# A two-layer Mamba, attention and expert network: instructions ordered by a planner inside the kernel, pairs of scan states added on GpSimd, expert weights in shared buffers

## The chip, the cores and the metric

The kernel runs on one core of one Trainium2 chip. The core has five engines that run side by side, each with an instruction queue that is worked off in order: TensorE (PE, the matrix unit), VectorE (DVE), ScalarE (ACT), GpSimd (POOL) and SyncE (SP), which here only issues DMA transfers. The time is the device time of one execution in microseconds. Three runs of the kernel before gave 986.20, 989.38 and 991.23 us; their median, 989.38 us, is the time to beat.

## What is computed

The input `x` is (4, 512, 128): four batches of 512 tokens with 128 features. Every part is added to its own input:

```python
x = x + L0_attn(layernorm(x), ...)   # selective scan, then attention and a gated FFN
x = x + L0_ffn(layernorm(x), ...)    # 128 -> 512 -> 128, ternary weights, exact gelu, layernorm
x = x + L1_attn(layernorm(x), ...)   # a second selective scan
x = x + L1_ffn(layernorm(x), ...)    # router with top 1 of 8 experts, 128 -> 2 x 512 -> 128
```

The selective scan appears twice per batch, once in each layer. It projects x to 256 inner channels and a gate of the same width, convolves four steps in time, and then runs a recurrence for 256 channels times 16 states:

```python
h = exp(delta_t * A) * h + delta_t * B_t * x_t      # h: 256 channels x 16 states
y_t = sum over the 16 states of h * C_t
```

`y` gets a skip term, is multiplied by `silu(gate)` and projected back to 128 features. In the expert layer every token goes through the one expert with the highest router probability, and the result is multiplied by that probability.

## The kernel before

**Layout.** A batch lies as four tiles of 128 tokens, or transposed as 128 features by 512 tokens. The 256 inner channels are two chunks of 128 partitions. Both layers' scans go through `scan_states` (L455), four batches times two layers: eight scans.

**One scan** is 16 jobs, a job being one chunk and two states (`NG = 2`). A job is fed by `feed` (L463): TensorE spreads the row B of each state over 128 partitions into a PSUM tile `b_n` (L469; the weight is one column of `sel`, broadcast), ScalarE makes `decay = exp(delta * A)` (L473), and SP loads the two rows of C, spread over 128 partitions, into `rep` (L478; 512 KB each). Then VectorE multiplies `b_n` by `du` (L509) and runs the recurrence as one scan instruction per state into `hs` (L510). GpSimd multiplies the pair by C in one instruction of 128x1024 (L511). At last `drain` (L485) sums over the states: TensorE multiplies each of the two halves of `hs` by the identity matrix and accumulates in the PSUM tile `y` (L494), one float32 matmul of 512 columns per state. Such a matmul is two passes in the trace, so 256 of them show as 512 records. `drain` of job k-1 stands behind the recurrence of job k, and it is held behind the last `spread` matmul by `issue_after`. The buffers are 3 for `b_n`, 3 for `decay`, 3 for `rep`, 3 for `hs` and 1 for `y`.

**The other stages** of a batch are generators: `front0` and `front1` (norm, transposition, convolution, gate, delta), `first` (the end of scan 0, then attention over four heads with 12 groups of query tiles), `dense` (gated FFN, then the ternary FFN), `second` (the end of scan 1, router). Batches 0 and 1, and 2 and 3, form two groups. For a group, `sort` gives every token a row in a DRAM table so that each expert's tokens fill whole tiles of 128, and writes the tokens there by eight indirect DMAs from the GpSimd queue (L783). `experts` then goes through 15 tiles: load a tile `xg` (L801), read the number of its expert into an SP register (L804), load its weights as `w_up`, 512 KB with two buffers, and `w_dn`, 256 KB with three (L809), normalise, transpose, multiply, and write the rows back with one indirect DMA (L832). The weight loads are held behind the last load of `rep`.

**The order of the work.** `run` gives each generator a due time and a length in units of one scan (scan 0 of batch b is due at b, scan 1 at 4+b, attention of b at b+1, and so on), and `issue` (L909) always advances the generator that is due first. This writes the program in one order; the framework's scheduler, with its own durations, then moves instructions within each engine's queue. Some of its freedom is taken away by hand: `behind` (issue after another instruction), `when` (wait for another instruction), and a hand-placed load of the exponential table on ScalarE at the end of each convolution (L408). ScalarE holds the tables for one set of functions at a time. Exp and Ln share a set here; Silu and Gelu each need another.

Of the kernel before, what the change touches and what calls it, by code (L numbers as in the profile page):

```python
# [8 lines left out]
F32 = mybir.dt.float32  # L9
# [9 lines left out]
P = 128  # L19
# [34 lines left out]

class Net:


    def __init__(self, ctx, tc, a, out):
        self.tc, self.nc, self.a, self.out = tc, tc.nc, a, out
        pool = lambda name, bufs, **k: ctx.enter_context(tc.tile_pool(name=name, bufs=bufs, **k))  # L60
# [13 lines left out]
    def c(self, name, shape, dtype=F32):  # L74
        return self.const.tile(shape, dtype, tag=name, name=name)

    def t4(self, name, bufs=None):
        return self.tok.tile([P, NT, D], F32, tag=name, name=name, bufs=bufs)

    def ft(self, name, shape, bufs=None, tag=None):  # L80
        return self.feat.tile(shape, F32, tag=tag or name, name=name, bufs=bufs)
# [4 lines left out]
    def behind(self, ins):  # L86
        return nullcontext() if ins is None else self.tc.issue_after(ins.ins)

    def when(self, done, ins):

        self.tc.add_manual_dep(
            ins.ins, done.ins.name,
            mybir.DependencyInfo(mybir.DependencyClass.Sync, mybir.DependencyReason.DATA),
        )

    def mm(self, name):
        return self.p_mm.tile([P, T], F32, tag="mm", name=name)

    def mm4(self, name):
        return self.p_mm.tile([P, NT, D], F32, tag="mm", name=name)  # L100

    def sm(self, name, shape, bufs=None):
        return self.small.tile(shape, F32, tag=name, name=name, bufs=bufs)
# [15 lines left out]
    def setup(self):  # L119
# [6 lines left out]
        make_identity(nc, self.ident)  # L126
# [32 lines left out]
    def setup_rest(self):  # L159
# [3 lines left out]
        make_causal_mask(nc, self.causal, mask_val=NEG)  # L163
# [69 lines left out]
        self.sorted = []  # L233
        for k, rows in enumerate(GROUPS):
            n = len(rows) * NT + E - 1
            d = self.dram.tile([n * P, XW], F32, tag=f"sorted{k}", name=f"sorted{k}", bufs=1)
            for j in range(0, n, NX):
                m = min(NX, n - j)
                nc.sync.dma_start(
                    out=d[j * P:(j + m) * P, :].rearrange("(j p) d -> p j d", p=P), in_=zero[:, :m, :]  # L240
                )
            self.sorted.append(d)
# [57 lines left out]
    def load_x(self, b):  # L300
        self.rows_x[b] = self.tok.tile([P, NT, XW], F32, tag="x", name=f"x_{b}", bufs=B)
# [50 lines left out]
    def rmsnorm(self, name, x, behind=None):  # L352
# [6 lines left out]
        with self.behind(behind):  # L359
            for t in range(NT):  # L360
                nc.scalar.activation(y[:, t, :], x[:, t, :], AF.Identity, scale=r[:, t:t + 1])
# [16 lines left out]
    def front(self, b, layer, x, scale=None):  # L378
# [10 lines left out]
        conv, gate = [], []  # L389
        for c in range(NB):  # L390
            ps = self.mm("conv_ps")
            for k in range(KC):
                last = nc.tensor.matmul(  # L393
                    ps, lhsT=taps[:, k, c * P:(c + 1) * P], rhs=xpad[:, k:k + T],
                    start=(k == 0), stop=(k == KC - 1),
# [4 lines left out]
        for c, ps in enumerate(conv):  # L400
            self.when(last, nc.scalar.activation(xs[:, c, :], ps, AF.Silu, bias=cb[:, c:c + 1]))
        for c in range(NB):
            ps = self.mm("z_ps")
            last = nc.tensor.matmul(ps, lhsT=wz[:, c * P:(c + 1) * P], rhs=xT, start=True, stop=True)
            gate.append(ps)
        for c, ps in enumerate(gate):
            self.when(last, nc.scalar.activation(sz[:, c, :], ps, AF.Silu))
        self.tc.keep_in_program_order(nc.scalar.preload_act_table_set("natural_log_exp_and_others"))  # L408
# [10 lines left out]
        cd = self.dram.tile([NS, T], F32, tag="cd", name="cd")  # L419
        nc.sync.dma_start(out=cd, in_=crow[32:32 + NS, :])  # L420

        parts = self.feat.tile([P, T], BF16, tag="parts", name="parts")
# [32 lines left out]
    def scan_states(self, b, layer):  # L455
# [7 lines left out]
        def feed(k):  # L463
# [3 lines left out]
            for i in range(NG):  # L467
                t = self.p_b.tile([P, T], F32, tag="b_n", name="b_n")
                spread = nc.tensor.matmul(t, lhsT=self.sel[:, n + i:n + i + 1].to_broadcast([P, P]), rhs=parts, start=True, stop=True)  # L469
# [7 lines left out]
            rep = self.scan.tile([P, NG, T], F32, tag="rep", name="rep", bufs=3)  # L477
            self.rep = nc.sync.dma_start(  # L478
# [4 lines left out]
            self.spread = spread  # L483

        def drain(k):  # L485

            c, n = jobs[k]
            if n == 0:
                y[c] = self.p_y.tile([P, T], F32, tag="y", name="y")
                nc.tensor.matmul(y[c], lhsT=skip[:, c, :], rhs=xs[:, c, :], start=True, stop=False)  # L490
            hs = done[k]
            with self.behind(self.spread):
                for i in range(NG):
                    nc.tensor.matmul(  # L494
                        y[c], lhsT=self.ident, rhs=hs[:, i, :],
                        start=False, stop=(n + i == NS - 1),
                    )
# [5 lines left out]
        for k, (c, n) in enumerate(jobs):  # L503
# [3 lines left out]
            hs = self.scan.tile([P, NG, T], F32, tag="hs", name="hs", bufs=3)  # L507
# [3 lines left out]
            nc.gpsimd.tensor_tensor(hs, hs, rep, ALU.mult)  # L511
            done[k] = hs
            if k >= 1:
                drain(k - 1)
            yield
        drain(len(jobs) - 1)
# [16 lines left out]
    def front0(self, b):  # L533
        with self.behind(self.backs.get(self.fronts - 2)):
            self.h[b], x = self.two_norms(self.x[b])
# [6 lines left out]
    def back0(self, b):  # L542
        h = self.h[b]
        self.backs[len(self.backs)] = self.nc.vector.tensor_tensor(h, h, self.back(b, 0), ALU.add)

    def attention(self, b):
        nc = self.nc
        h = self.h[b]
        x = self.rmsnorm("a", h, self.last_head)
# [20 lines left out]
        for tiles in ((0, 1), (2,), (3,)):  # L570
            for hd in range(HEADS):
# [6 lines left out]
                last = turned[-4] if len(turned) >= 4 else None  # L578
                for n, i in enumerate(tiles):
                    nk, k0 = (i + 1) * P, at[n] * P  # L580
                    with self.behind(last):
                        nc.tensor.matmul(  # L582
# [394 lines left out]
```

## Time and profile before

The profiled execution took 989.92 us, of which the span from its first to its last instruction is 988.1 us.

| engine | busy us | share of span | what it mostly does |
|---|---|---|---|
| PE | 807.4 | 82% | 281.1 us of it are the matmuls of `hs` by the identity (L494) |
| DVE | 660.1 | 67% | recurrence 302.4 us (L510), product by `du` 168.1 us (L509) |
| ACT | 572.1 | 58% | decay 177.6 us (L473), 100 table loads of 1283 ns |
| POOL | 460.1 | 47% | `hs` by C 305.7 us (L511) |
| DMA | | 30.3% of 16 engines | 102.24 MB, 103 GB/s in the mean |

A busy share says how long an engine had an instruction in work, not that it set the pace. Matmuls overlap each other and their weight loads (PEld), and the mean duration of one is longer than the distance between two starts. The granted TensorE clock was 0.911 of full speed in the mean.

The trace splits into six stretches, which are used below: 0 to 50 us (loads and the first front part, before the first recurrence at 50.5 us), 50 to 150 us (scans and front parts only), 150 to 640 us (attention and dense parts beside the scans), 640 to 750 us (the last front parts and the sorting of the first group), 750 to 890 us (the last scans beside the experts of the first group), and from 890 us on (router and experts of the second group, alone).

### The profile page before, as it was taken

How to read it: one execution, taken by the hardware profiler on the slowest of the kernel's cores; microseconds unless marked ns; L12 is line 12 of the kernel's file. 1: busy time of each engine (PE TensorE's matmuls, PEld its weight loads, DVE VectorE, ACT ScalarE, POOL GpSimd, SP SyncE). 2: the span in 40 equal slices, each digit the busy share in tenths (PEclk: the TensorE clock that was granted, in tenths of full speed). 3: DMA queues.
4: the chain of work that ended last, by engine and by line, in shares of the span. 5: the costliest groups of instructions: out<-in, count | busy, mean ns of one | idle time of the engine just before them, and what ended most of it. 6: DMA issues, size and time to landing. Idle time of an engine off the chain costs nothing. (4 is left out here: it accounts for less than half of the span.)

```text
span 988.1 us, 10337 instructions
## 1 busy us (share of the span) xinstructions
PE 807.4 (82%) x3242; PEld 450.1 (46%) x3242; DVE 660.1 (67%) x1111; ACT 572.1 (58%) x938; POOL 460.1 (47%) x305
## 2 busy tenths in 40 slices
PE   3876779997899988999989989789585987982685
PEld 1322244443444554544644446344332555641675
DVE  2399876876668586678774768757666878872122
ACT  4474356745669566686674864568445666841332
POOL 4256752553534454336442444444455845663122
PEclk9978989998899799998998979899797998995799
DMA  5236421222212121121320212121025574732463
GB/s 147 76 109 171 144 87 66 85 107 85 86 49 99 46 86 64 65 87 64 107 75 33 79 50 98 73 86 66 30 97 175 176 233 145 230 99 75 160 217 113
DMA packets 44084, 102.24 MB, mean 103 GB/s; under 512 B 6660, under 2 KB 18912, under 8 KB 44030
## 3 DMA queue, kind: packets, MB, share of 16 engines
q1 hardware_dynamic: 42558, 99.45, 30.3%
q0 software_dynamic: 1472, 2.14, 0.6%
q8 instruction: 25, 0.41, 0.2%
q14 instruction: 29, 0.24, 0.1%
HBM read 97.14 MB, written 5.34 MB: 104 GB/s over the span
## 5 line engine op out<-in xcount | busy, mean ns | idle before, releaser
L511 POOL TENSOR_TENSOR hs<-hs,rep 128x1024 f32<-128x1024 f32 x128 | 305.7, 2389 | 313.8 <-DVE hs L510 156.4
L510 DVE TENSOR_TENSOR_SCAN hs<-decay,b_n 128x512 f32<-128x512 f32 x256 | 302.4, 1207 | 3.6 <-ACT decay L473 1.8
L494 PE MATMUL y<-hs,ident 128*128 128x512 f32 x512 | 281.1, 662 | 13.1 <-POOL hs L511 13.1
L473 ACT ACTIVATE decay<-delta,nega 128x511 f32<-128x511 f32 x256 | 177.6, 717 | 111.1 <-DVE hs L510 89.2
L509 DVE TENSOR_TENSOR b_n<-b_n,du 128x512 f32<-128x512 f32 x256 | 168.1, 687 | 44.8 <-PE b_n L469 35.5
L494 PEld LDWEIGHTS y<-hs,ident 128*128 128x128 f32 x512 | 100.9, 210 | 129.1 <-issue 82.0
L469 PE MATMUL b_n<-parts,sel 128*128 128x512 bf16 x256 | 92.1, 408 | 61.2 <-DVE hs L510 56.8
L393 PE MATMUL conv_ps<-xpad,taps 128*128 128x512 f32 x128 | 62.7, 619 | 3.1 <-ACT xpad L374 2.6
L855 DVE TENSOR_TENSOR sa<-sa,g_ps 128x512 f32<-128x512 f32 x30 | 20.5, 684 | 66.3 <-PE g_ps L852 59.2
L591 ACT ACTIVATE pr<-s_ps,nm 128x128 f32<-128x128 f32 (+2 forms) x64 | 33.5, 524 | 53.8 <-DVE nm L590 52.5
L832 POOL DMA_INDIRECT out<-yj,xg x30 | 29.9, 996 | 63.0 <-DVE yj L829 60.3
L602 PEld LDWEIGHTS tp<-v,pT 128*128 128x128 f32 x320 | 43.6, 203 | 32.8 <-ACT pT L598 19.4
L369 PE MATMUL tp<-ident,ln 128*128 128x128 f32 x96 | 25.0, 335 | 37.5 <-ACT ln L330 20.8
L582 PE MATMUL s_ps<-kT,qT 32*128 32x128 f32 (+3 forms) x128 | 55.1, 511 | 0.0
L469 PEld LDWEIGHTS <-sel 128*128 128x128 bf16 x256 | 26.5, 107 | 58.1 <-issue 56.4
L602 PE MATMUL tp<-v,pT 128*128 128x33 f32 x320 | 45.6, 285 | 2.1 <-ACT pT L598 2.1
L369 PEld LDWEIGHTS tp<-ident,ln 128*128 128x128 f32 x96 | 14.3, 160 | 66.1 <-ACT ln L330 22.3
L595 PEld LDWEIGHTS tp<-ident,pr 128*128 128x128 f32 x160 | 21.0, 152 | 50.1 <-ACT pr L591 39.0
L845 PE MATMUL a_ps<-xj,w_up 128*128 128x128 f32 x240 | 36.4, 297 | 8.9 <-ACT xj L817 8.7
L811 ACT ACTIVATE xn<-xg 128x128 f32<-128x128 f32 x30 | 14.8, 494 | 48.8 <-DMA xg<-sorted 48.6
L595 PE MATMUL tp<-ident,pr 128*128 128x128 f32 x160 | 32.0, 303 | 13.0 <-ACT pr L591 12.5
L590 DVE TENSOR_REDUCE nm<-s_ps 128x1 f32<-128x128 f32 (+2 forms) x64 | 30.7, 479 | 17.3 <-PE s_ps L585 15.5
(201 smaller groups left out, 1254.1 us busy)
## 6 DMA issues: line engine op xcount, KB each, us to landing
rep<-cd SPq DMA_DIRECT2D x128, 512.0 KB, 3.6
w_up<-in_w_rows SPq DMA_DIRECT2D x30, 512.0 KB, 4.5
w_dn<-in_w_rows SPq DMA_DIRECT2D x30, 256.0 KB, 4.5
xg<-sorted SPq DMA_DIRECT2D x30, 66.0 KB, 2.3
sorted<-zero SPq DMA_DIRECT2D x2, 726.0 KB, 8.6
x<-in_x SPq DMA_DIRECT2D x4, 256.0 KB, 4.4
raw_cw<-in_cw_rows SPq DMA_DIRECT2D x2, 512.0 KB, 4.6
sorted<-zero SPq DMA_DIRECT2D x2, 264.0 KB, 10.1
```

The lines of the kernel that those rows point to most:

```text
L369: nc.tensor.transpose(ps[:, t * P:(t + 1) * P], x[:, t, :], self.ident)
L393: last = nc.tensor.matmul(ps, lhsT=taps[:, k, c * P:(c + 1) * P], rhs=xpad[:, k:k + T], start=(k == 0), stop=(k == KC - 1),)
L469: spread = nc.tensor.matmul(t, lhsT=self.sel[:, n + i:n + i + 1].to_broadcast([P, P]), rhs=parts, start=True, stop=True)
L473: nc.scalar.activation(da[:, i, 1:], delta[:, c, 1:], AF.Exp, scale=neg_a[:, c * NS + n + i:c * NS + n + i + 1],)
L494: nc.tensor.matmul(y[c], lhsT=self.ident, rhs=hs[:, i, :], start=False, stop=(n + i == NS - 1),)
L509: nc.vector.tensor_tensor(b, b, du[:, c, :], ALU.mult)
L510: nc.vector.tensor_tensor_scan(hs[:, i, :], da[:, i, :], b, 0.0, ALU.mult, ALU.add)
L511: nc.gpsimd.tensor_tensor(hs, hs, rep, ALU.mult)
L582: nc.tensor.matmul(ps[:, k0:k0 + nk], lhsT=qT[hp, i * P:nk], rhs=kT[hp, :nk], start=True, stop=False)
L595: last = nc.tensor.transpose(tp[:, j * P:(j + 1) * P], pr[:, j * P:(j + 1) * P], self.ident)
L602: nc.tensor.matmul(tp[:, n * w:(n + 1) * w], lhsT=pT[:, (at[n] + j) * P:(at[n] + j + 1) * P], rhs=v[:, j, g, :], start=(j == 0), stop=(j = ...
L845: nc.tensor.matmul(pa[:, f, :], lhsT=w[0][:, f * P:(f + 1) * P], rhs=xj, start=True, stop=True)
```

## The change

Three things are edited; the arithmetic is otherwise the same.

1. **The planner.** `self.nc` is now a recorder. Every call is kept as an `Op` with its engine, the boxes of the tiles it reads and writes, and a duration by a formula in `Plan.cost`. A tile is a `Slot` in a ring of buffers that is only made when its first instruction is emitted. When everything is collected, `Plan.order` plays all five queues forward: of the first 60 ready instructions of each engine it takes the one that can start first (within 0.1 us, the one with the earlier due time), allowing for free buffers, for 1.35 us at a change of function table, and for DMA at 200 GB/s. `Plan.issue` emits in that order; the framework's scheduler is switched off for all engines but GpSimd, whose instructions are chained one behind the other, except for a group of indirect DMAs of one kind. The hand-made `behind`, `when` and the hand-placed table load go; a table load is emitted where the planned order changes the set. Where the recorder counts instructions, ScalarE has 57 table loads instead of 100, all other counts of the old instructions on TensorE, VectorE and ScalarE are as before save for those of point 2, and SP has 90 weight loads instead of 60.
2. **Pairs of states.** After the multiplication by C, GpSimd adds the second half of `hs` to the first (128 new instructions of 128x512), and TensorE accumulates one matmul per job instead of two. `hs` has 4 buffers instead of 3, and job k is drained in its own step.
3. **Expert weights.** `w_up` and `w_dn` lose buffers of their own. The two halves of the first weight (256 KB each, two loads instead of one) use the buffers of attention's `pT`, now 4 instead of 3, and the second weight those of `pr` (4).

In addition the convolution waits for the end of the scan two front parts earlier (`after=back`), where before the norm ahead of it stood behind that instruction, and the counting matmuls of `sort` wait for the router's last choice.

```diff
+    def cost(self, engine, what, out, ins, args, k):
+        n = width(out)
+        m = max([n] + [width(v) for v in ins])
+        if engine == "tensor":
+            if what == "transpose":
+                return 0.112
+            half = k["rhs"].slot.dtype == BF16 if isinstance(k["rhs"], View) else False
+            return max(0.11, n * 0.00042) if half else 2 * max(0.112, n * 0.000836)
+        if engine == "scalar":
+            scalars = sum(isinstance(k.get(x), View) for x in ("bias", "scale", "accum_out"))
+            return 0.21 + n * 0.00083 + 0.1 * scalars
+        if engine == "vector":
+            if what == "tensor_tensor_scan":
+                return 0.2 + n * 0.002
...
+            return 0.19 + m * 0.001
+        if engine == "gpsimd":
+            if ALU.pow in args:
+                return 1.15
+            return 0.3 + n * (0.00215 if what == "tensor_tensor" else 0.001)
+        return 0.45
...
+            best = None
+            for e, ops in ready.items():
+                found = []
+                for op in ops[:60]:
+                    at = room(op)
+                    if at is None:
+                        continue
+                    at = max(at, op.at, free[e])
+                    if op.table and op.table != table:
+                        at += self.SWITCH
+                    found.append((at, op))
+                if found:
+                    first = min(f[0] for f in found)
+                    at, op = next(f for f in found if f[0] <= first + 0.1)
+                    if best is None or at < best[0]:
+                        best = at, op
...
             hs = done[k]
-            with self.behind(self.spread):
-                for i in range(NG):
-                    nc.tensor.matmul(
-                        y[c], lhsT=self.ident, rhs=hs[:, i, :],
-                        start=False, stop=(n + i == NS - 1),
-                    )
+            nc.tensor.matmul(y[c], lhsT=self.ident, rhs=hs[:, 0, :], start=False, stop=(n + NG == NS))
...
-            hs = self.scan.tile([P, NG, T], F32, tag="hs", name="hs", bufs=3)
+            hs = self.scan([P, NG, T], F32, tag="hs", name="hs", bufs=4)
...
             nc.gpsimd.tensor_tensor(hs, hs, rep, ALU.mult)
+            nc.gpsimd.tensor_tensor(hs[:, 0, :], hs[:, 0, :], hs[:, 1, :], ALU.add)
             done[k] = hs
-            if k >= 1:
-                drain(k - 1)
+            drain(k)
...
-            w = self.ft("w_up", [P, 2 * EF], bufs=2), self.ft("w_dn", [P, EF], bufs=3)
-
-            with self.behind(self.rep):
-                for part, name in zip(w, ("w1_rows", "w2_rows")):
-                    nc.sync.dma_start(out=part, in_=self.a[name][bass.ds(e, 1)].rearrange("o p n -> (o p) n"))
+            w = []
+            for name, at, tag in (("w1_rows", 0, "pT"), ("w1_rows", EF, "pT"), ("w2_rows", 0, "pr")):
+                part = self.ft("w_" + name, [P, EF], bufs=4, tag=tag)
+                get = nc.add(
+                    "sync", lambda p=part, n=name, at=at: weights(p, n, at, e), [part], [], 0.45, after=[e]
+                )
+                get.bytes = 4 * P * EF
+                w.append(part)
```

## The prediction

> **What bounds the kernel now.** No engine is full over the whole span (PE 82%, DVE 67%), so the first view is the busy time of each engine by stretch. Columns: length, then busy us (instructions) of PE, PEld, DVE, ACT and POOL, then clock, DMA share and GB/s.
>
> ```profile
> 0.00:50.00 50.00, 30.41 (x71) 13.76 (x72) 17.02 (x50) 23.35 (x42) 18.00 (x48) 1.00 0.37 110
> 50.00:150.00 100.00, 73.15 (x184) 31.37 (x184) 88.22 (x113) 51.05 (x87) 60.94 (x31) 0.86 0.41 130
> 150.00:640.00 490.00, 445.04 (x1716) 237.13 (x1715) 349.06 (x604) 318.28 (x540) 219.86 (x122) 0.92 0.21 75
> 640.00:750.00 110.00, 85.86 (x293) 42.09 (x292) 71.48 (x128) 65.44 (x95) 51.87 (x33) 0.91 0.22 76
> 750.00:890.00 140.00, 115.35 (x568) 74.53 (x566) 112.63 (x159) 89.02 (x126) 85.62 (x46) 0.94 0.54 177
> 890.00:988.10 98.10, 57.57 (x417) 51.27 (x417) 21.69 (x63) 25.01 (x53) 23.81 (x25) 0.82 0.45 142
> ```
>
> TensorE sets the pace for half of the kernel: from 150 to 640 us it is busy 445.0 of 490 us, 91%, while DVE has 71% and POOL 45%. From 50 to 150 us it is DVE (88%). From 750 to 890 us PE and DVE share it (82% and 80%). From 640 to 750 us nothing is above 78%: the work waits for chains. After 890 us there is one chain only.
>
> The groups by cost say what this work is (after the bar: busy us and mean ns of one; then the idle time of the engine before it).
>
> ```profile
> L511 POOL TENSOR_TENSOR hs<-hs,rep 128x1024 f32<-128x1024 f32 x128 | 305.7, 2389 | 313.8 <-DVE hs L510 156.4
> L510 DVE TENSOR_TENSOR_SCAN hs<-decay,b_n 128x512 f32<-128x512 f32 x256 | 302.4, 1207 | 3.6 <-ACT decay L473 1.8
> L494 PE MATMUL y<-hs,ident 128*128 128x512 f32 x512 | 281.1, 662 | 13.1 <-POOL hs L511 13.1
> L509 DVE TENSOR_TENSOR b_n<-b_n,du 128x512 f32<-128x512 f32 x256 | 168.1, 687 | 44.8 <-PE b_n L469 35.5
> ```
>
> A third of PE's time is L494, which only sums. POOL waits 313.8 us before L511: it has room. DVE waits only 44.8 us before L509.
>
> **The change, part by part.**
>
> *Half of L494 goes.* 256 of its 512 records, at 281.1/512 = 0.549 us of busy time each, are 140.5 us: 20.1 in 50–150, 77.8 in 150–640 (half of 155.6 us in that stretch), 14.7 in 640–750, 27.9 in 750–890. Where PE sets the pace, the next bound is what is late next.
>
> *128 adds on POOL.* L645 is the same operation and shape:
>
> ```profile
> L645 POOL TENSOR_TENSOR x<-x,h x4: 1262/1263/1267, 275.4 to 658.7; 128x512 f32<-128x512 f32 x4
> L510 DVE TENSOR_TENSOR_SCAN hs<-decay,b_n x256: 1184/1209/1222, 50.5 to 883.4; 128x512 f32<-128x512 f32 x128
> L509 DVE TENSOR_TENSOR b_n<-b_n,du x256: 668/689/700, 49.3 to 881.6; 128x512 f32<-128x512 f32 x128
> L297 DVE SCALAR_TENSOR_TENSOR tern_fc<-raw_fc,thr_fc,low_fc x1: 2812/2812/2812, 39.2 to 39.2; 128x512 f32<-128x512 f32 x1
> ```
>
> 128 x 1.263 = 161.7 us. By jobs in each stretch (20, 69, 13, 26) POOL becomes 86, 307, 68 and 118 us. A job then costs POOL 2.39 + 1.26 = 3.65 us and DVE 2 x (0.687 + 1.207) = 3.79 us: nearly equal. The add also lies between recurrence and `y`; with four `hs` buffers it delays `y`, not the next job, as long as POOL's queue keeps up.
>
> *A rule against this.* The Trainium skill (Perfetto Trace Analysis, Optimizing Scalar/DVE Operations) warns that GpSimd and DVE share an SBUF read port, so moving work between them may not help. If each add held off DVE for its length, DVE would rise by 161.7 us to 822 us, and the gain would be gone. The four rows above decide: recurrence and product hardly vary (1184 to 1222 ns, 668 to 700 ns) although POOL is busy half of the time; both read one operand from PSUM. L297, two operands from SBUF, took 2.81 us where its twin for the other weight took 0.72. It started 0.1 us after a 2.35 us POOL instruction. So only the few DVE instructions with two SBUF operands pay: over L256, L297, L348, L446 and L449 the excess over their shortest is some 11 us. With POOL busy about 70% instead of half in the middle I add 5 us (0 to 15), and not 161.7.
>
> *Table loads.* ACT has 43 fewer, at 1.283 us: 55 us less of 572. ACT is no bound (65% from 150 to 640), so I count nothing by itself; the attention chain gets shorter, which helps to reach the next bound. Worth 0 to 15 us.
>
> *The planner.* Its durations stand close to the rows: recurrence 1.22 us (trace 1.207), product 0.70 (0.687), `hs` by C 2.50 (2.389), add 1.40 (1.263), table 1.35 (1.283). One is short: a float32 matmul of 512 columns is 0.856 us, while the trace has 2 x 0.549 = 1.10 us. The order is fixed, so where PE is late all wait in turn, but a late matmul doesn't change how much work there is. No row prices an order. Bounds: the share of its bound engine that today's order reaches, 91% on PE and 88% on DVE at best, and 80% where two engines are near the bound (750–890).
>
> *The clock rule.* The Trainium skill (TensorE: Matmul & The Clock Gate, What's actually happening) says that the array runs at half rate until it has been busy, and falls back after an idle window of about 3.4 us. An idler PE would then be slower. The rows agree in sign: clock 0.92 at 91% busy, 0.86 at 73%. PE in 150–640 is 445.0 - 77.8 = 367 us at 0.92, and 367 x 0.92/0.86 = 393 us at 0.86. I take 0.89: 379 us.
>
> *Expert weights.* Same bytes, 30 more issues; an issue of L809 is 0.33 us with some 0.2 us between, so 16 us on SP's queue, beside transfers of 4.5 us. Two tiles of first weights are in flight as before. In the last part, eleven reads of expert numbers (0.43 us each, 4.7 us) now stand in SP's queue ahead of the loads of `xg`; the eight scatter DMAs that these wait for take 10 us anyway, which hides them. If SP came late, each of 30 tiles would pay up to 0.5 us: 15 us. I take 0.
>
> *The convolution's new wait* (`after=back`) stands on PE; what would queue behind it are spreads of `b_n`. Before, the same condition held the norm ahead of it. I take 0 (at worst some 4 us for each of six front parts).
>
> *The sum by stretch.*
> - 0–50: the same chain of norm, convolution, delta: 50.
> - 50–150: DVE stays at 88, POOL rises to 86: 100.
> - 150–640: PE 379, DVE 349 + 3, POOL 307. At 91% of PE it is 416; at 80%, for three near-equal engines, 474; at 91% of PE without loss of clock 403. Near the first, since the third engine has still 25% free: 418.
> - 640–750: all three near 70 us of work; between 71.5/0.88 = 81 and today's 110: 98.
> - 750–890: POOL 118 is the bound now; 118/0.88 = 135, today's 140 the other end: 137.
> - From 890: PE stands 0.55 to 0.65 us per tile waiting for `xj` and longer for `xg`; the built order has transpositions of later tiles ahead of their turn. Up to 14 us to win, none for sure: 92.
>
> Together 895, with the 1.8 us around the span (989.92 - 988.1) **897 us**. The profiled execution stands 0.5 us above the median, so it is the forecast for the median too. From 50 to 890 us this asks DVE to be busy (621.4 + 5 + 5)/753 = 84%, where the second 5 us are spare; it has 74% now.
>
> **The rivals.**
>
> *A. The planner is better than that.* DVE has 88% from 50 to 150 us; at 88% throughout, 631/0.88 = 717, with 50 + 90 + 2: **859 us**. For it: durations near the rows, 43 table loads gone. Against it: three engines close to their limit.
>
> *B. Most of PE's relief is not used.* DVE reaches only 78%: 631/0.78 = 809, with 50 + 94 + 2: **955 us**. For it: PE's duration in the plan is short, and the attention chain leaves DVE waiting for PE and ACT. Against it: nothing else gets longer.
>
> *C. Slower: POOL's queue becomes the chain.* POOL now has `hs` by C, the add, the powers of the norms (1.03 us each) and the scatter DMAs in one fixed order. The view of waits:
>
> ```profile
> POOL hs L511 <- DVE hs L510: 156.4, 62, 11.8
> POOL hs L511 <- issue: 45.7, 10, 13.5
> POOL out L832 <- DVE yj L829: 60.3, 17, 13.2
> ```
>
> From 50 to 890 us POOL is busy 418.3 and idle 421.7 us, 3.3 us per job. With the adds it is busy 580. If it kept three quarters of its idle time, because something that waits stands at the head of its queue, the middle would take 580 + 316 = 896: **1046 us**. It decides from 260 us of idle time on (840 - 580), 2.0 us per job. For it: a scatter that waits for `yj` holds up the next pair. Against it: most of that idle time is POOL waiting for DVE because it is early, which shrinks as DVE speeds up.
>
> *D. It doesn't do what it says.* The built order has 128 matmuls L494 instead of 256 and 128 adds more on POOL; only a cancelling gain could leave the time as it is.
>
> **How the numbers follow.** Forecast (870 to 930) 0.55, A 0.17, B 0.13, no change (within 0.5%, some 5 us, about what a measurement of this kernel can tell from none) 0.03, C 0.12. Faster: 0.55 + 0.17 + 0.13 = 0.85. The range goes from 838 (DVE at 90% and the tail at 84) to 968 (B and a little more), and leaves out C, the last of A and of B, 0.18.
>
> **What would show it.** PE busy near 670 us and below 85% in the attention stretch; POOL near 620; recurrence still 1.2 us and product 0.69 (else the port rule was right); ACT near 520; clock between 0.86 and 0.92; DVE the busiest in the scans, its idle time down from 219 us to about 120 between first and last recurrence. The forecast is wrong if POOL waits longer before an `hs` than DVE before a `b_n` while `hs` buffers are full, or if PE, at 80% or less, is still what DVE waits for.

## The result and the profile after

The changed kernel took **978.79 us** (median of 4 runs, 974.61 to 979.34); the kernel before, run beside it on the same chip, 989.85 us (986.20 to 991.23). The ratio is **0.9885** with a 95% interval of 0.9846 to 0.9923: 1.2% faster, where the forecast was 897 us. The profiled execution took 978.41 us, its span is 976.2 us, and the mean granted clock 0.831 (before 0.911). Two of the four executions of e5, n1 and e14 below, and one of e8, took over 1.5% longer than the fastest of their kernel, at a lower granted clock, and all times below are medians of the others (e5: 948.50 us, where a text written before a run has 956).

First the page of the changed kernel: busy time by engine, the granted clock in 40 slices, and groups of instructions. Every recorded instruction carries the line of the emitting call, L199, so groups are told apart by their tiles.

```profile
PE 758.1 (78%) x2969; PEld 432.9 (44%) x2986; DVE 706.8 (72%) x1111; ACT 515.9 (53%) x895; POOL 624.9 (64%) x433
PEclk9955678959998697999879967688977988875798
L199 POOL TENSOR_TENSOR hs<-hs,rep 128x1024 f32<-128x1024 f32 x128 | 303.1, 2368 | 122.1 <-issue 50.7
L199 DVE TENSOR_TENSOR_SCAN hs<-decay,b_n 128x512 f32<-128x512 f32 x256 | 311.9, 1219 | 17.3 <-POOL r L199 0.5
L199 PE MATMUL y<-hs,ident 128*128 128x512 f32 x256 | 171.4, 759 | 32.7 <-POOL hs L199 29.9
L199 DVE TENSOR_TENSOR b_n<-b_n,du 128x512 f32<-128x512 f32 x256 | 173.9, 680 | 13.2 <-PE b_n L199 4.1
L199 POOL TENSOR_TENSOR hs<-hs 128x512 f32<-128x512 f32 x128 | 166.7, 1302 | 9.4
```

Half of the summing matmuls are gone, as are 43 table loads of ACT, and the adds are there at 1.30 us. But PE's busy time fell by 49 us only, from 807.4 to 758.1, and DVE's rose by 47, from 660.1 to 706.8. The clock row has eight slices of 5 or 6; the kernel before has one.

Then the busy times of each engine in three stretches of the changed kernel, cut at the first and the last recurrence (columns as in the prediction).

```profile
0.00:54.60 54.60, 37.40 (x89) 17.43 (x90) 26.86 (x76) 31.37 (x52) 21.03 (x50) 0.98 0.54 149
54.60:865.60 811.00, 657.09 (x2456) 361.80 (x2473) 657.15 (x972) 460.30 (x792) 572.34 (x354) 0.83 0.29 99
865.60:976.20 110.60, 63.63 (x425) 53.68 (x424) 22.84 (x64) 24.26 (x53) 31.54 (x30) 0.76 0.40 126
```

In the kernel before, the same three were 50.5, 834.0 and 103.6 us, with DVE busy 619.8 us in the middle one. So 23 us were won between the recurrences, and 11 were given back ahead of and behind them. PE and DVE are now busy equally long in the middle, 657 of 811 us or 81%, and neither is full. The same view in steps of 50 us shows how they share the time.

```profile
50.00:100.00 50.00, 29.11 (x41) 7.68 (x39) 47.98 (x50) 23.34 (x33) 42.37 (x22) 0.56 0.25 85
150.00:200.00 50.00, 45.79 (x157) 22.91 (x157) 29.99 (x50) 26.53 (x47) 27.22 (x14) 0.86 0.15 53
350.00:400.00 50.00, 35.01 (x90) 15.36 (x91) 47.32 (x63) 25.34 (x55) 45.14 (x30) 0.80 0.34 120
400.00:450.00 50.00, 48.25 (x199) 25.80 (x200) 34.91 (x65) 37.57 (x61) 25.95 (x17) 1.00 0.17 59
```

The two engines take turns. Where no attention runs (50 and 350 us), DVE is busy 96% and 95%, and PE, with 41 and 90 matmul records, has a clock of 0.56 and 0.80. Where attention runs (150 and 400 us), PE is busy 92% and 96%, and DVE 60% and 70%. The planned order bunches the attention: of its 160 matmuls of `v` with `pT`, counted in the trace between each 16 recurrences that DVE starts (eight scan jobs), the third to eleventh group hold 0, 40, 6, 34, 0, 9, 31, 12, 28; in the kernel before 6, 26, 11, 18, 19, 18, 22, 9, 31. The matmuls that were removed belong to scan jobs, and many of those now stand where PE has time to spare.

**DVE's 47 us.** The sum of single durations rose by 23.2 us, from 728.0 to 751.2; the other 23.5 us are overlap lost between neighbours. The largest part of the first is the product of mean and deviation in every norm, a 128x4 instruction with two operands in SBUF. Its row in the trace, before (min/median/max in ns):

```profile
L328 DVE SCALAR_TENSOR_TENSOR nm_r<-mv,r x20: 139/163/176, 14.9 to 709.7; 128x4 f32<-128x4 f32 x20
```

and after, with the row of the recurrence beside it:

```profile
L199 DVE SCALAR_TENSOR_TENSOR nm_r<-mv,r x20: 152/164/2310, 12.7 to 708.9; 128x4 f32<-128x4 f32 x20
L199 DVE TENSOR_TENSOR_SCAN hs<-decay,b_n x256: 1189/1221/1222, 54.6 to 864.4; 128x512 f32<-128x512 f32 x128
```

Together they went from 2.9 to 15.3 us of busy time. Eleven of the 20 are as short as before. Each of the nine long ones starts while a POOL instruction is running and ends 0.01 to 0.03 us after it; the short ones meet none, or start ahead of it or less than 0.02 us behind its start. One of them (start, length):

```profile
364.89 1.26 POOL L199 TENSOR_TENSOR hs<-hs 128x512 f32<-128x512 f32 x1
365.28 0.89 DVE L199 SCALAR_TENSOR_TENSOR nm_r<-mv,r 128x4 f32<-128x4 f32 x1
```

The add ends at 366.15 us, the product at 366.17. The longest, 2.31 us, stands beside a POOL product of 2.45 us (`delta` by `sp_e`). The recurrence, which reads PSUM, keeps its 1.22 us. The second part is seen in the timeline (start, length, then the instruction; neighbours of one kind are one line, x2). Of the kernel before:

```profile
82.47 1.26 DVE L509 TENSOR_TENSOR b_n<-b_n,du 128x512 f32<-128x512 f32 x2
83.65 2.31 DVE L510 TENSOR_TENSOR_SCAN hs<-decay,b_n 128x512 f32<-128x512 f32 x2
85.89 1.19 DVE L446 SCALAR_TENSOR_TENSOR du<-du,sp_e 128x1024 f32<-128x1024 f32 x1
```

Two products and two recurrences take 85.89 - 82.47 = 3.42 us, 1.71 per state. After:

```profile
369.94 0.67 DVE L199 TENSOR_TENSOR b_n<-b_n,du 128x512 f32<-128x512 f32 x1
370.71 1.22 DVE L199 TENSOR_TENSOR_SCAN hs<-decay,b_n 128x512 f32<-128x512 f32 x1
371.85 0.68 DVE L199 TENSOR_TENSOR b_n<-b_n,du 128x512 f32<-128x512 f32 x1
```

One product and the recurrence that needs it take 371.85 - 369.94 = 1.91 us per state. In DVE's order before, two products are neighbours 87 times; in the planned order twice. Before, a recurrence behind two products starts 0.09 us ahead of the second one's end (median of 74 places); after, behind a single product, it starts 0.10 us after the product's end (212 places). These gaps are not busy time: the idle time before the recurrence, 3.6 us in the prediction's row, is 17.3 us in the row above. Of the 23.5 us of lost overlap, 11.5 lie between products and recurrences, the rest between DVE's other instructions.

**The tail.** POOL's timeline at the last scan of the changed kernel, with PE's summing matmuls:

```profile
861.04 1.02 PE L199 MATMUL y<-hs,ident 128*128 128x512 f32 x2
...
864.35 1.22 DVE L199 TENSOR_TENSOR_SCAN hs<-decay,b_n 128x512 f32<-128x512 f32 x1
...
868.89 1.01 POOL L1075 DMA_INDIRECT out<-yj,xg  x1 [0.15 <-issue]
869.93 2.35 POOL L199 TENSOR_TENSOR hs<-hs,rep 128x1024 f32<-128x1024 f32 x1
872.36 1.26 POOL L199 TENSOR_TENSOR hs<-hs 128x512 f32<-128x512 f32 x1
...
873.68 2.07 PE L199 MATMUL y<-hs,ident 128*128 128x512 f32 x2 [2.81 <-POOL hs L199]
875.79 0.69 DVE L199 TENSOR_TENSOR xs<-sz,y 128x512 f32<-128x512 f32 x1 [10.22 <-PE y L199]
```

POOL is a job and a scatter behind: its last add ends at 873.6 us, 8.0 us after the last recurrence (865.6). Before, its last product ended 2.6 us after it. DVE waits 10.2 us. The same pair of matmul records takes 1.02 us at 861 and 2.07 us at 874, after gaps.

### The profile page after: what moved, and what is told of

Read it like the earlier page. It is cut to its first block, busy times and chain, and to the rows that moved or that the text cites. A ratio compares the mean times of both kernels' runs of the same rounds, so it can differ in the third digit from the quotient of the medians.

```text
span 976.2 us, 10032 instructions
## 1 busy us (share of the span) xinstructions
PE 758.1 (78%) x2969; PEld 432.9 (44%) x2986; DVE 706.8 (72%) x1111; ACT 515.9 (53%) x895; POOL 624.9 (64%) x433
## 5 line engine op out<-in xcount | busy, mean ns | idle before, releaser
L199 POOL TENSOR_TENSOR hs<-hs,rep 128x1024 f32<-128x1024 f32 x128 | 303.1, 2368 | 122.1 <-issue 50.7
L199 DVE TENSOR_TENSOR_SCAN hs<-decay,b_n 128x512 f32<-128x512 f32 x256 | 311.9, 1219 | 17.3 <-POOL r L199 0.5
L199 ACT ACTIVATE decay<-delta,nega 128x511 f32<-128x511 f32 x256 | 178.4, 718 | 157.1 <-DVE hs L199 154.4
L199 PE MATMUL y<-hs,ident 128*128 128x512 f32 x256 | 171.4, 759 | 32.7 <-POOL hs L199 29.9
L199 PE MATMUL b_n<-parts,sel 128*128 128x512 bf16 x239 | 104.4, 455 | 107.9 <-DVE hs L199 107.2
L199 DVE TENSOR_TENSOR b_n<-b_n,du 128x512 f32<-128x512 f32 x256 | 173.9, 680 | 13.2 <-PE b_n L199 4.1
L199 POOL TENSOR_TENSOR hs<-hs 128x512 f32<-128x512 f32 x128 | 166.7, 1302 | 9.4
L199 PEld LDWEIGHTS y<-hs,ident 128*128 128x128 f32 x256 | 52.9, 230 | 130.7 <-POOL hs L199 103.5
L199 PEld LDWEIGHTS <-sel 128*128 128x128 bf16 x256 | 29.3, 115 | 92.4 <-issue 90.9
L199 PE MATMUL s_ps<-kT,qT 32*128 32x128 f32 (+3 forms) x128 | 62.1, 569 | 1.3 <-ACT kT L199 1.1
L199 PE MATMUL conv_ps<-xpad,taps 128*128 128x512 f32 x128 | 61.9, 622 | 0.0
L199 DVE TENSOR_TENSOR sa<-sa,g_ps 128x512 f32<-128x512 f32 x30 | 20.2, 678 | 50.5 <-PE g_ps L199 25.1
L199 PEld LDWEIGHTS tp<-v,pT 128*128 128x128 f32 x320 | 47.4, 220 | 19.7 <-issue 7.9
L199 DVE TENSOR_REDUCE nm<-s_ps 128x1 f32<-128x128 f32 (+2 forms) x64 | 30.2, 484 | 28.8 <-PE s_ps L199 27.1
L199 ACT COPY pT<-tp 128x384 f32<-128x384 f32 (+1 forms) x48 | 24.2, 517 | 47.7 <-PE tp L199 47.6
L199 PE MATMUL tp<-v,pT 128*128 128x33 f32 x320 | 47.9, 296 | 1.4 <-ACT pT L199 1.4
L199 POOL TENSOR_TENSOR delta<-delta,sp_e 128x1024 f32<-128x1024 f32 x8 | 19.6, 2451 | 39.0 <-ACT delta L199 27.7
L199 DVE RECIPROCAL rs<-tp 128x1 f32<-128x1 f32 (+1 forms) x48 | 7.9, 164 | 50.3 <-PE tp L199 39.1
L199 PE MATMUL w_ps<-w_w_rows,sa 128*128 128x128 f32 x240 | 35.9, 288 | 8.1 <-DVE sa L199 6.6
L199 ACT ACTIVATE pr<-s_ps,nm 128x128 f32<-128x128 f32 (+2 forms) x64 | 31.4, 523 | 19.2 <-DVE nm L199 11.5
```

Source lines behind the costliest of these rows:

```text
L199: emit = lambda: getattr(getattr(self.nc, engine), what)(*[real(v) for v in args], **{n: real(v) for n, v in k.items()})
```

## The experiments

A null edit changes no work, only a number of the planner. Theory after the result: PE's relief is worth next to nothing because VectorE sets the pace where the removed matmuls stood; the planned order makes VectorE's work 47 us longer, and bunches the attention. Rivals: the added POOL work is what costs; the shared weights cost; the planner's parameters (tolerance, PE's durations) are wrong.

| run | what differs | us | ratio to before |
|---|---|---|---|
| e1_pairs_only | before + pairs | 1059.09 | 1.0704 [1.0653, 1.0755] |
| e2_plan_only | after - pairs | 984.09 | 0.9965 [0.9948, 0.9983] |
| e3_tol1 | after, tolerance 1.0 | 981.90 | 0.9939 [0.9907, 0.9971] |
| n2_switch | after, null edit | 966.30 | 0.9782 [0.9750, 0.9814] |
| e16_shared_hs3 | after, `hs` and `pT` 3 | 972.53 | 0.9841 [0.9804, 0.9878] |
| e12_own_hs3 | the same, own weight buffers | 980.40 | 0.9892 [0.9861, 0.9924] |
| e15_nmr | after, mean x deviation on POOL | 969.69 | 0.9793 [0.9758, 0.9828] |
| e5_ttfirst | after, products ahead | 948.50 | 948.50/987.21 = 0.961, two executions |
| n1_ttfirst_switch | e5, null edit | 950.14 | 0.9621 [0.9554, 0.9689] |
| e6_ttfirst_tol1 | e5, tolerance 1.0 | 954.77 | 0.9687 [0.9659, 0.9716] |
| e7_ttfirst_pe | e5, PE's planned durations longer | 940.22 | 0.9532 [0.9493, 0.9570] |
| e9_ttfirst_blank | e5 + 128 matmuls | 955.77 | 0.9721 [0.9685, 0.9758] |
| e8_ttfirst_nmr | e5 + e15 | 924.86 | 0.9387 [0.9358, 0.9416] |
| e14_ttfirst_nmr_switch | e8, null edit | 942.13 | 0.9523 [0.9476, 0.9570] |
| e11_ttfirst_nmr_nopair | e8 - pairs | 937.39 | 0.9488 [0.9453, 0.9522] |
| e10_ttfirst_nmr_pe | e8 + e7 | 971.41 | 0.9827 [0.9790, 0.9864] |

### The parts alone: pairs without the planner, the planner without pairs

```diff
# before, pairs only
             nc.gpsimd.tensor_tensor(hs, hs, rep, ALU.mult)
+            nc.gpsimd.tensor_tensor(hs[:, 0, :], hs[:, 0, :], hs[:, 1, :], ALU.add)
...
-                for i in range(NG):
-                    nc.tensor.matmul(
-                        y[c], lhsT=self.ident, rhs=hs[:, i, :],
...
+                nc.tensor.matmul(
+                    y[c], lhsT=self.ident, rhs=hs[:, 0, :], start=False, stop=(n + NG == NS),
+                )
```

> The kernel before with only the pair adds (128 adds on GpSimd, one matmul of hs per job instead of two); the old scheduler, three hs buffers, own weight buffers. Clock theory (with fewer matmuls the granted clock falls, and what is left of TensorE's work takes longer): clock falls from 0.91 to 0.83 to 0.86, time 965 to 985 us. Order theory (the planner's rule is what spoils the gain): without the planner the pairs bring most of what was forecast, 900 to 930 us. Port theory (adds on GpSimd lengthen VectorE's instructions with two SBUF operands): VectorE busy 15 to 25 us more than before's 660.

> The changed kernel without the pair adds: planner and shared weight buffers, two matmuls of hs per job as before. Clock theory: clock back at 0.90 to 0.92, TensorE busy near 800 us, time 970 to 1000 us, so that the pairs were worth little under the planner too. Order theory: the planner alone is slower than before, 1000 to 1030 us, because it bunches attention. Port theory: VectorE busy 15 to 25 us less than the 707 of the changed kernel; product and recurrence still alternate, so it stays above 680.

Pairs alone make the old order 7% slower, the planner alone 0.35% faster. None of the three theories had 1059 us for the pairs; the clock was 0.814, and DVE was busy 668.3 us, 8 more than before. With the planner alone the clock was 0.924 and PE busy 802.8 us, as the clock theory said, but DVE 698.0 us, 9 less than with the pairs and not 15 to 25. So the adds cost DVE 8 or 9 us of busy time in either order, and 38 of its 47 us come with the planned order. The view of waits of the kernel before (who waited for whom: us, times, longest):

```profile
PEld y L494 <- POOL hs L511: 34.3, 25, 4.0
PE y L494 <- POOL hs L511: 13.1, 12, 2.5
```

and of the pairs-only kernel:

```profile
PEld y L493 <- POOL hs L510: 137.0, 64, 5.5
PE y L493 <- POOL hs L510: 63.4, 44, 3.9
```

PE's queue is worked off in order: a `y` matmul whose pair POOL has not finished holds up the matmuls behind it, and with the adds the pair comes later. That this makes the 72 us is argued from these rows; PEld and PE run at the same time, so the two don't add up. Pairs in the old order with four `hs` buffers were not tried. In the changed kernel the same waits are 103.5 and 29.9 us, and the adds cost nothing like it: 984.1 against 978.8 us puts the gain of the pairs at 5 us, less than a null edit moves (next section).

### Planner parameters and null edits

```diff
-                    at, op = next(f for f in found if f[0] <= first + 0.1)
+                    at, op = next(f for f in found if f[0] <= first + 1.0)
```

> The changed kernel with the planner's tolerance at 1.0 us instead of 0.1: among instructions that can start within 1 us of the first, the one due first is taken, so attention and scans are spread more evenly. Order theory: 930 to 960 us, and fewer stretches of 25 us in which VectorE is above 93% while TensorE is below 75%. Clock and port theories: no change beyond 1%, 970 to 985 us.

No gain, where the order theory had 930 to 960. In the same count the attention is more even than in the changed kernel (18, 22, 15, 25, 9, 31, 9, 31 from the third group on), and the time is the same. How far a planned order varies by itself was measured with an edit that changes no work:

```diff
-    SWITCH = 1.35
+    SWITCH = 1.28
```

> The changed kernel with the same edit alone (table change at 1.28 us instead of 1.35). If orders are a matter of chance: more than 10 us off 979, either way. If not: 973 to 985.

> Products recorded ahead of recurrences (956 us), and as an edit that should not matter the planner's price of a table change at 1.28 us, the trace's value, instead of 1.35. It measures how much the time moves when the planned order is merely drawn anew. Theory that all differences of 15 us between planned orders are chance: 935 to 975, more than 10 us off 956. Theory that the edits themselves act: 950 to 962.

It moved the changed kernel by -12.5 us, the one with the products ahead by +1.6, and the best one (below) by +17.3. **Two planned orders can differ by 12 to 17 us for no reason that a person chose**; differences up to that size below are not read as effects.

### Products ahead of recurrences

```diff
             for i, b in enumerate(b_n):
                 nc.vector.tensor_tensor(b, b, du[:, c, :], ALU.mult)
+            for i, b in enumerate(b_n):
                 nc.vector.tensor_tensor_scan(hs[:, i, :], da[:, i, :], b, 0.0, ALU.mult, ALU.add)
```

> The changed kernel with the two products of a job recorded ahead of its two recurrences, which makes them neighbours on VectorE (product after product 99 times instead of 2). Theory that alternating dependent instructions cost VectorE time: busy time falls from 707 to about 685 us and the time by 10 to 20 us, to 958 to 970. Order theory alone: no change, 972 to 985.

> Products recorded ahead of recurrences, and the planner's tolerance 1.0 us instead of 0.1. Order theory (attention bunched by the earliest-start rule still costs time once VectorE's pairs are restored): 925 to 945 us. If bunching costs nothing: 950 to 962, as with the products ahead alone (956).

> Products recorded ahead of recurrences, and TensorE's planned durations raised to what the trace has at its mean clock (float32 matmul of 512 columns 1.075 us instead of 0.856, transposition 0.14 instead of 0.112). Theory that the short durations make the other engines wait in the wrong order: 930 to 945 us. If not: 950 to 962.

Two products are neighbours 99 times instead of twice. DVE is busy 691.2 instead of 706.8 us, and its idle time before the recurrence falls from 17.3 to 1.8 us:

```profile
L199 DVE TENSOR_TENSOR_SCAN hs<-decay,b_n 128x512 f32<-128x512 f32 x256 | 300.9, 1205 | 1.8
```

Together that frees 31 us of DVE's time, and the kernel is 30.3 us faster (978.79 - 948.50). All eight kernels with pairs and the products ahead lie between 925 and 971 us, mean 948.5; the six planned ones with pairs and without that lie between 966 and 982, mean 975. The groups overlap only in the slowest of the eight, and a draw of the order doesn't explain 26 us between their means. The tolerance again does nothing, though it makes the attention more even (18, 22, 15, 25, 13, 27 against 12, 28, 0, 21, 19, 24 from the third group on). Longer planned durations for PE (1.05 instead of 0.84 ns per column and pass) gave 940, but together with the next edit 971, so that no gain of theirs is shown.

### Is PE's relief worth anything?

The kernel with the products ahead, with a second matmul per job, whose weight is zero. It adds nothing to `y` and gives PE the removed work back.

```diff
-            nc.tensor.matmul(y[c], lhsT=self.ident, rhs=hs[:, 0, :], start=False, stop=(n + NG == NS))
+            nc.tensor.matmul(y[c], lhsT=self.ident, rhs=hs[:, 0, :], start=False, stop=False)
+            nc.tensor.matmul(y[c], lhsT=self.blank, rhs=hs[:, 0, :], start=False, stop=(n + NG == NS))
```

> Products recorded ahead of recurrences, and one more matmul of 512 columns per job with weights of zero, which adds nothing to y but gives TensorE back the work that the pair adds took from it. Clock theory (the falling clock gives back the gain of the removed matmuls): clock 0.91 to 0.93 instead of 0.859, and time within 1% of 956 us. If the removed work is a gain that something else eats: 975 to 1000 us.

955.77 us with the work, 948.50 without it (two executions, 943.04 and 953.97; the two profiled ones took 954.83 and 953.97). The first scan-only stretch and the middle, without the added matmuls (50 to 150 and 150 to 640 us):

```profile
50.00:150.00 100.00, 61.32 (x136) 20.97 (x134) 92.95 (x106) 46.31 (x80) 91.10 (x54) 0.75 0.33 111
150.00:640.00 490.00, 428.77 (x1645) 238.12 (x1655) 364.11 (x611) 314.11 (x555) 302.48 (x192) 0.87 0.21 73
```

and with them:

```profile
50.00:150.00 100.00, 69.41 (x172) 26.70 (x171) 95.39 (x107) 46.96 (x80) 91.46 (x53) 0.89 0.31 111
150.00:640.00 490.00, 452.88 (x1770) 245.36 (x1782) 368.67 (x607) 302.83 (x541) 304.06 (x192) 0.95 0.21 72
```

PE does 125 matmul records more in the middle (1770 against 1645) at a clock of 0.95 instead of 0.87, and DVE is busy 369 us instead of 364. So the removed matmuls are worth some 7 us by these medians, less than a null edit moves. Whether because the lower clock takes back what they free, or because they stood where DVE sets the pace, these runs don't separate: the rows show both the clock and DVE's 93 to 95% from 50 to 150 us.

### Held VectorE instructions, and the best version

```diff
-        nc.vector.scalar_tensor_tensor(off, mean, -1.0, r, ALU.mult, ALU.mult)
+        nc.gpsimd.tensor_tensor(off, mean, r, ALU.mult)
+        nc.gpsimd.tensor_scalar(off, off, -1.0, None, ALU.mult)
```

> The changed kernel, with only the mean times deviation of each norm moved from VectorE to GpSimd (two small instructions in place of one; they are 20). If held small VectorE instructions cost the time what they cost VectorE in busy time, it takes 979 - 12 = some 967 us, with the row of that product gone. If the gain of e8_ttfirst_nmr was a shorter norm chain, it can be more, 940 to 960. If the time is a draw of the planned order, anything from 950 to 985 is possible and the row says nothing of it.

> Products recorded ahead of recurrences, and the product of mean and reciprocal deviation (two SBUF inputs, 128x4, 24 times) computed on GpSimd in two instructions instead of one on VectorE. Port theory: VectorE loses the instructions that GpSimd held off for up to 2.3 us, its busy time falls from 691 by 10 to 18 us, and the time by 3 to 12 us, to 944 to 953. If the held-off time is hidden: 953 to 960.

> The best version (products ahead, mean times deviation on GpSimd) with the planner's price of a table change 1.28 instead of 1.35 us, which changes no work. If its two edits make the gain: 925 within 15 us. If 925 was a lucky planned order: 940 to 970, as for the other versions with the products ahead.

> The three edits together: products ahead of recurrences, mean times deviation on GpSimd, TensorE's planned durations as in the trace. If each acts by itself: 956 - 31 - 16 = 909 us. If the two later ones were draws of order: 920 to 950.

> Products ahead of recurrences and mean times deviation on GpSimd, without the pair adds (two matmuls of hs per job). Clock theory (the pairs are worth next to nothing, since the clock gives back what they save): clock 0.92 or more, 920 to 940 us, within 15 us of the 925 with the adds. If the pairs are worth more once VectorE's losses are gone: 950 to 985.

Alone (e15), DVE's busy time falls by 10.7 us to 696.1, and the kernel by 9.1 us, near the 12 that were expected, though a draw of the order could do that too. On POOL the two instructions, 20 of each, take 0.205 and 0.238 us. With the products ahead it gives the fastest kernel of all, **924.86 us**, 6.1% below before. But DVE's busy time fell from 691.2 to 686.3 us only, where 10 to 18 were expected, and that doesn't make 23.6 us of time. Its null edit gives 942.13: part of the 925 is a lucky order, and the mean of the two draws, 933.5, is the fairer figure. Without pairs the same kernel takes 937.39, so the pairs are worth nothing that can be seen beside the draws of the order. All three edits together (e10) took 971.41 us, where the sum of their single gains gave 909.

### Shared weights and the fourth `hs`

```diff
-            for name, at, tag in (("w1_rows", 0, "pT"), ("w1_rows", EF, "pT"), ("w2_rows", 0, "pr")):
-                part = self.ft("w_" + name, [P, EF], bufs=4, tag=tag)
+            for name, at, tag, bufs in (("w1_rows", 0, "w_up", 4), ("w1_rows", EF, "w_up", 4), ("w2_rows", 0, "w_dn", 3)):
+                part = self.ft("w_" + name, [P, EF], bufs=bufs, tag=tag)
```

> The changed kernel with 3 buffers instead of 4 for hs and for the attention's pT, weights still sharing. It is the partner of e12_own_hs3. If a fourth hs buffer carries the longer GpSimd chain, it is slower than 979 by 10 us or more; if VectorE and TensorE set the pace in turns, 979 within 15 us.

> As e16_shared_hs3, but the expert weights have buffers of their own again (first weight four halves, second weight three). If sharing holds weight loads back until the attention is done with its tiles, or the attention until the experts are, this is faster than e16_shared_hs3 by more than 15 us; if sharing costs nothing, the two agree within 15 us.

Both have 3 `hs` and 3 `pT`. Own buffers are not faster (980.4 against 972.5 us), and a fourth `hs` buffer is not either (978.8 against 972.5, where `pT` has one more too). Each difference is within a draw of the order, and neither rival shows.

## Why the prediction was wrong in size

The direction was right; 81 us were missed (span 976.2 against a sum of 895), and the time lies above the range. Cut at the recurrences, with the forecast's tail of 92 from 890 us counted from the last recurrence (103.6 before, less the 6.1 us that it expected to win, 97.5), the sum has 50 + 747.5 + 97.5; measured were 54.6 + 811.0 + 110.6. So 4.6 us were missed ahead, 63.5 in the middle, 13.1 behind.

**The step that failed is the sum from 150 to 640 us.** It turned 77.8 us of removed matmuls into 72 us of time (490 to 418), with DVE's work longer by 3 us and the planned order put at nothing. Put back, the removed matmuls of the whole kernel cost some 7 us (e9), and DVE's work between the first and the last recurrence grew by 37 us, of which 29 stand in the kernel with the planner alone (e2: 648.3 against 619.8 us).

- **VectorE's work, the largest mis-sized term.** The sum gave it 5 us more (0 to 15), all for the adds, and the adds do cost 8 or 9. What it left out came with the planned order. The middle has 37 us more (657.2 against 619.8), and the whole 47. At the forecast's own share of 83.6% (624.8 of 747.5), 657.2 us make 786: 39 of the 63.5 us. Half of the 47 is longer single instructions. For these the prediction had the right mechanism in the large rows but looked past the 128x4 ones, which in the trace of before never went over 176 ns. The other half is lost overlap, 11.5 us of it where product and recurrence alternate, and was not in the sum at all: its 3.79 us per job adds the two means, where the timeline of before has 3.42 at one place. The alternation could have been read in the built order. The run with the products ahead showed its worth: 30.3 us, 26 in the means of the groups.
- **The bound share in the middle.** The sum put PE at 379 us and full for 91% from 150 to 640 us, "near the first" of its bounds. PE was busy 420 of these 490 us at a clock of 0.84, and DVE 366 us. The share of 81% instead of 83.6% accounts for the other 25 us. Some 14 of them are the longer idle time before the recurrence (3.6 to 17.3 us). The cause of the rest stays open. DVE's waits for PE in the attention (`rs` and `nm`) did not shrink: 60.9 us before, 70.2 after, between the first and the last recurrence. The bunching of attention is no shown cause: e3 and e6 are more even and not faster, and the fastest kernel (e8) has 3, 37, 9, 31, 6, 30, 7, 21, 16.
- **PE's relief.** The term of 140.5 us in records was right (256 records went), but PE's busy time fell by 49 us, to 758.1 and not near 670: the records of `y` that are left take 759 instead of 662 ns in the mean. What it bought, some 7 us, is less than a null edit moves. The clock of 0.89 was too high. The rule of the Trainium skill (TensorE: Matmul & The Clock Gate, What's actually happening), that an idle array falls to half rate, was weighed with one row of 0.86 at 73% busy; after, a stretch with PE 58% busy had 0.56, nearly the rule's half. The rule's window of idle time is shown by no run here.
- **The tail** was forecast to get 6 us shorter and got 7 longer; 5.4 of those are POOL's last job, which comes 8.0 instead of 2.6 us after the last recurrence. The planned kernels without pairs, e2 and e11, have a tail of 104 us. Nothing was won in the expert loop.
- **Ahead of the first recurrence** 4.6 us were lost; why was not tried.
- **POOL**: 624.9 us against some 622, adds of 1.30 against 1.263 us: right. **ACT**: 515.9 against 517: right, and as forecast no gain by itself is seen. **Expert weights** at nothing: borne out within the draws.
- **The port rule**: the blanket charge of 161.7 us was rightly refused (recurrence 1.219, product 0.680 us). What decides is stated more exactly in the skill's page SBUF — State Buffer (section "SBUF: two separate sides"): an instruction of VectorE with two operands in SBUF and a GpSimd instruction that reads SBUF exclude each other for the whole length of the one that starts first. The nine long 128x4 products, each of which ends just behind a POOL instruction that started first, agree with it.
- **The rivals.** B (most of PE's relief unused, 955 us) was the nearest in mechanism; its DVE share was too low (78%) and its DVE work too small. C, POOL's longer chain as the bound, did not come with the planner, where POOL's waits for issue stayed near where they were (45.7 before, 50.7 after); but pairs alone in the old order ended slower, at 1059, and there PE's waits for POOL grew most. That C's 1046 came near it is luck: the place was PE's queue and not POOL's.
- **The signs named ahead.** POOL, ACT, recurrence and product came as said. PE's 670 us (758.1), its share below 85% in the attention stretch (86%), a clock of 0.86 or more (0.831) and an idle time of DVE near 120 us (153.9) did not. POOL waited longer before an `hs` (122.1 us) than DVE before a `b_n` (13.2), as the first sign of being wrong had it; whether the `hs` buffers were full, these rows don't say. And DVE's longest waits in the middle were for PE, at 81% busy, where the second sign says 80% or less.

## What to carry to other kernels

Work taken off an engine is worth what that engine holds up where the work stood; put it back as empty work, and the time says whether it was worth anything. When work is moved to an engine that shares a port with the busiest one, count all its instructions with two operands in SBUF, the smallest too, at the length of what can hold them. When an automatic order decides, read the built order for neighbours that depend on each other, and measure a null edit before crediting any edit of a few per cent.

## What the runs showed of the hardware

- A 128x4 product of two SBUF operands on DVE takes 0.16 us, or up to 2.31 us beside POOL. In e8, where it is moved away, three other instructions with two SBUF operands are longer: `du`, `sp_e` and `delta` of 128x1024 take 2.21, 2.15 and 2.21 us in the mean instead of 1.74, 1.73 and 1.46 in e5, 1.46, 1.82 and 1.83 after and 1.69, 1.22 and 1.37 before. That the move made them longer is not shown.
- Two independent neighbours on DVE overlap more than two that depend on each other: 1.71 against 1.91 us per state for the same two instructions, and a recurrence starts 0.09 us ahead of the end of the product before it where two products stand in a row, and 0.10 us behind it where one does (medians, before and after).
- The same two matmul records of one job took 1.02 us and, 13 us later and after gaps, 2.07 us; the granted clock of a stretch fell to 0.56 where PE was 58% busy.
